# Sums over scan directions beside the dense convolutions: cut into pieces of two matmuls, spread over more half units, and charged to the TensorE budget of each half unit

## The chip, the cores and the metric

The kernel runs on one core of a Trainium2 chip. The metric is device time in microseconds (us), the median of several executions; lower is better. TensorE is called PE here, VectorE DVE, ScalarE ACT, GpSimd POOL, and SP is SyncE, which issues the DMAs.

## The reference, cut to what matters

Two layers of a vision network work on 8 images of 64 x 64 pixels and 192 channels, in float32. Layer 0 is a depthwise convolution, a chunked state-space scan in two directions and an MLP. Layer 1 splits the channels into halves: the left half goes through dense 3x3 convolutions, the right half through a selective scan in four directions over 192 inner channels with 16 states each:

```python
        # layer 1, left half
        y = _conv(_bn1(xl), conv1_w, conv1_b)
        y = _conv(relu(_bn2(y)), conv2_w, conv2_b)
        xl_out = relu(_conv(relu(_bn3(y)), conv3_w, conv3_b))
        ...
        # layer 1, right half: one recurrence for each of 4 directions, 192 channels, 16 states
        h = jnp.exp(d_t[..., None] * A) * h + (d_t * u_t)[..., None] * b_t[:, :, None, :]
        ys = einsum(h, c_t) + Ds * xs4
        yv = ys[:, 0] + jnp.flip(ys[:, 2], -1) + wh2hw(ys[:, 1]) + wh2hw(jnp.flip(ys[:, 3], -1))
        xr_out = einsum(_ln(yv) * silu(z), out_proj_w)
```

`yv`, the sum over the four directions with the skip term `Ds * xs4`, is what the change is about. `wh2hw` turns a plane walked by columns into one walked by rows.

## The kernel before

**The spine.** `selective_scan` (L1300 on) walks 3072 *units*, 384 for each image. A unit is one tile of 128 partitions (8 channels by 16 states) and 1024 tokens. For each unit SP fetches `dA` (L1435, 512 KB, six units ahead, seven buffers), ACT takes its exponential (L1440, two or three units ahead), PE spreads the inputs into `dB` in PSUM (L1448, two matmuls, two buffers), DVE weighs `dB` (L1465) and runs the scan instruction (L1472), POOL multiplies by C (L1475), and for every four units PE gathers the states into `acc` (L1486), which ACT copies to `y` (L1491). All of this is pinned: every engine takes its instructions in the order in which the Python code emits them, and SP's DMA issues stand in one queue in that order too.

**Work beside the spine.** All other work of an image is written as generators. A generator's `yield` of a number says how much TensorE work was just emitted (about one microsecond for 1.0, 1.2 for a 128x512 float32 matmul); a `yield None` says that nothing more of this generator is to be emitted in this half unit. `Beside.half()` runs twice in each unit: it adds `rate` to `credit` and then runs the generator in front until the credit is used up or a `None` comes. `rate` is set once per image in `spread_over`, from the sum of all the stages' costs. The scan's own matmuls are taken off the credit too (`beside.spend`).

The stages stand in this order beside the scan of image b: `conv0`, `ssd`, `mlp0` of image b+1 (layer 0), `conv_branch` of image b-2 (left half of layer 1), `scan_outputs` of image b-2, then `scan_inputs` and `transposed` of image b+1, which write `u`, the scan inputs of the next image, to DRAM. In the middle of the last but one tile of an image (unit 744 of the program, where the image ends at 768) `beside.finish()` emits at once whatever is left. Right behind it SP issues the loads of the next image's `u` (L1349), and three units later PE starts `ps_xp` from them (L1362). For the last image the list is `conv_branch`, `scan_outputs`, `conv_branch`.

**The sums.** `scan_sums` is a *side* generator: `conv_branch` sets it as `cx.side`, and from then on every half unit runs it up to its next `None` (`cx.aside()`). It works on 128 channels and then on 64. For each it loads the plane that is walked by columns into `whole` (for 128 channels POOL adds a second one to it, L1162), and then for each of 8 blocks of 512 tokens it puts the sum into one PSUM bank: plain matmuls with the identity or the skip diagonal (L1183: three for 128 channels, two for 64) and one matmul that reads `whole` with its rows and columns exchanged (L1185). ACT copies the bank out (L1188) and SP stores it (L1190). In the kernel before, all matmuls of a block are emitted in one half unit, and what they cost is counted nowhere: `aside()` drops the numbers, and `conv_branch=190.0` is the cost of the convolutions alone (8 blocks of 19 matmuls at 1.2). Such a side generator runs for images 0 to 6; the sums of image 7 stand in `tail()`, behind the scan.

Of the kernel before, what the change touches and what calls it, by code (L numbers as in the profile page):

```python
# [56 lines left out]
def wh_to_hw(ap):  # L57

    return ap.rearrange("p (w h) -> p h w", w=WW)
# [16 lines left out]
class Shared:  # L76
# [15 lines left out]

    def aside(self):

        for piece in self.side or ():
            if piece is None:
                return True
        self.side = None
        return False

    def pool(self, name, bufs=1):

# [180 lines left out]
def pause(n):  # L283

    for i in range(n):
        yield None


def among(gen, calls, n=2):

    calls = list(calls)
    for i, cost in enumerate(gen):
        yield cost
        if i % n == n - 1 and calls:
            calls.pop(0)()
    for call in calls:
        call()
        yield None
# [10 lines left out]
def token_rows(rows, d, c, n):  # L309

    width = 1
    for v in rows.shape[1:]:
        width *= v
    out = []
    for half in range(2):
        if d == 0:
            at, step, chunk = c * Q + half * Q // 2, 1, Q  # L320
        else:
            at, step, chunk = c * Q // HH + half, WW, Q // HH
        out.append((at * width, [[step * width, Q // 2], [chunk * width, n]]))
    return out
# [548 lines left out]
def conv_branch(cx, xl, short, out, side=None):  # L873

    nc, pin, k = cx.nc, cx.pin, cx.k
    with cx.pool("cw1") as wp, cx.pool("a1", 2) as ap:
# [78 lines left out]
        def load_w(i, r):  # L955
            here = slice(3 * r, 3 * (r + 1))
            pin(nc.sync.dma_start(out=ws[i][:, here], in_=k[("conv1_w", "conv2_w")[i]][:, here]))
# [11 lines left out]
        cx.side = side  # L969
        turns = in_turn(range(NB), scale, first, wait, second, third, add, store)  # L970
        yield from among(turns, [lambda r=r: load_w(1, r) for r in range(3)])
        while cx.aside():
            yield None


# [150 lines left out]
def scan_sums(cx, y, u):  # L1126

    nc, pin, k = cx.nc, cx.pin, cx.k

    def slots(n):  # L1130
        for i in range(n):
            yield 1.0
            yield None

    def cols(r, n):
        return slice(r * n, (r + 1) * n)

    with cx.pool("t2") as tp:

        for size, firsts, seconds, v, skip, eye in (  # L1140
            (128, [p[0] for p in y], [p[1] for p in y], u[0], k["skip_a"], k["ident"]),
            (64, [p[2][0:64] for p in y], [p[2][64:128] for p in y], u[2][0:64], k["skip_b"], k["twice"]),
        ):
            whole = tp.tile([128, L], F32, tag="whole", name="whole")
            for q in range(4):
                here = cols(q, L // 4)
                pin(nc.sync.dma_start(out=whole[:size, here], in_=seconds[0][:, here]))
                if size < 128:
                    pin(nc.sync.dma_start(out=whole[size:, here], in_=seconds[1][:, here]))
                yield from slots(1)  # L1150
            if size < 128:
                yield from slots(1)
            else:
                others = []
                for q in range(NB + 1):
                    if q < NB:
                        others.append(tp.tile([128, 512], F32, tag="p1", name="p1", bufs=2))
                        pin(nc.sync.dma_start(out=others[q], in_=seconds[1][:, cols(q, 512)]))
                    yield from slots(3 if q == 0 else 1)
                    if q > 0:  # L1160
                        here = cols(q - 1, 512)
                        pin(nc.gpsimd.tensor_add(whole[:, here], whole[:, here], others[q - 1]))  # L1162

            def load(r):
                part = tp.tile([128, 512], F32, tag="part", name="part", bufs=3)
                pin(nc.sync.dma_start(out=part[:size], in_=firsts[0][:, cols(r, 512)]))
                vt = tp.tile([size, 512], F32, tag="vt", name="vt", bufs=2)
                pin(nc.sync.dma_start(out=vt, in_=v[:, cols(r, 512)]))
                if size < 128:
                    pin(nc.sync.dma_start(out=part[size:], in_=firsts[1][:, cols(r, 512)]))  # L1170
                    return part, [(eye, part), (skip, vt)]
                p1 = tp.tile([128, 512], F32, tag="p1", name="p1", bufs=2)
                pin(nc.sync.dma_start(out=p1, in_=firsts[1][:, cols(r, 512)]))
                return part, [(eye, part), (eye, p1), (skip, vt)]

            coming = load(0)
            yield from slots(4)
            for r in range(NB):
                (part, terms), coming = coming, load(r + 1) if r + 1 < NB else None
                yield from slots(1)  # L1180
                ps = cx.one("ps_sum")[:size]
                for i, (w, t) in enumerate(terms):
                    pin(nc.tensor.matmul(ps, lhsT=w, rhs=t, start=i == 0, stop=False))  # L1183
                rows = wh_to_hw(whole)[:, r * RB : (r + 1) * RB, :]
                pin(nc.tensor.matmul(ps.rearrange("p (h w) -> p h w", w=WW), lhsT=eye, rhs=rows, start=False, stop=True))  # L1185
                yield 0.6 * len(terms)
                yield None
                pin(nc.scalar.copy(part[:size], ps))  # L1188
                yield from slots(1)
                pin(nc.sync.dma_start(out=firsts[0][:, cols(r, 512)], in_=part[:size]))  # L1190


# [72 lines left out]
class Beside:  # L1265
# [13 lines left out]

    def half(self):  # L1280

        self.cx.aside()
        self.credit = min(self.credit, self.rate) + self.rate
        while self.credit > 0.0 and self.stages:
            for cost in self.stages[0]:
                if cost is None:
                    return
                self.credit -= cost
                if self.credit <= 0.0:
                    return  # L1290
            self.stages.pop(0)
# [277 lines left out]
@with_exitstack  # L1569
def vision_mamba_pair_kernel(ctx: ExitStack, tc: tile.TileContext, x: bass.AP, p0: dict, p1: dict, out: bass.AP):  # L1570

    B = x.shape[0]
    cx = Shared(tc)
    cp = ctx.enter_context(tc.tile_pool(name="c", bufs=1))
    dp = ctx.enter_context(tc.tile_pool(name="d", bufs=1, space=DRAM))
    d2 = ctx.enter_context(tc.tile_pool(name="d2", bufs=2, space=DRAM))
    x1 = dp.tile([B, C, L], F32, tag="x1", name="x1")
    cx.singles = [ctx.enter_context(tc.tile_pool(name="ps", bufs=4, space=PSUM))]
    with cx.pool("once") as tp:
        setup(cx, cp, dp, tp, p0, p1)  # L1580
    us, ys, xns = {}, {}, {}

    def short(b):

        return x1[b].rearrange("(i g) l -> g i l", g=2)

    def sums(b):
        return scan_sums(cx, ys[b], us[b])

    def outputs(b):  # L1590
        return scan_outputs(cx, ys[b][0], xns[b], short(b)[1], out[b][1])

    def branch(b, side=None):
        return conv_branch(cx, x1[b][0:CH], short(b)[0], out[b][0], side)

    def stages(b):

        if b < B:
            us[b] = [d2.tile([128, L], F32, tag=f"u{t}", name=f"u{t}") for t in range(3)]
            ys[b] = [[d2.tile([128, L], F32, tag=f"y{g}{t}", name=f"y{g}{t}") for t in range(3)] for g in range(2)]  # L1600
            xns[b] = d2.tile([CH, L], F32, tag="xn", name="xn")
            beside.add(conv0(cx, x[b]))
            beside.add(ssd(cx))
            beside.add(mlp0(cx, x[b], x1[b]))
        if b > 1:
            beside.add(branch(b - 2, sums(b - 2)))
            beside.add(outputs(b - 2))
        if b == B:
            beside.add(branch(b - 1))
        if b < B:  # L1610
            beside.add(scan_inputs(cx, x1[b][CH:C], xns[b], us[b]))
            beside.add(transposed(cx, us[b]))

    beside = Beside(cx)
    with tc.tile_pool(name="ps_a", bufs=4, space=PSUM) as more:
        cx.singles.append(more)
        stages(0)
        beside.finish()
        beside.costs.update(conv_branch=190.0, scan_outputs=78.0)
        cx.singles.remove(more)  # L1620

    def tail():
        beside.add(sums(B - 1))
        beside.add(outputs(B - 1))
        beside.finish()

    def start_image(b, halves):
        stages(b + 1)
        beside.spread_over(halves, 450.0)

    selective_scan(cx, lambda b: us[b], lambda b: ys[b], beside, B, start_image, tail)
# [95 lines left out]
```

## Time and profile before

| | |
|---|---|
| time, median of 3 executions | 16043.01 us (16030.84, 16043.01, 16072.04) |
| the profiled execution | 16027.31 us |
| its span, first to last instruction | 16025.4 us |
| PE busy | 12969.3 us (81%) |
| DVE busy | 12232.0 us (76%) |
| POOL busy | 10981.2 us (69%) |
| ACT busy | 9059.2 us (57%) |
| DMA engines busy (queue of SP) | 79.5% of 16 engines' span |
| mean granted TensorE clock | 0.854 |

How to read it: the profile gives for each group of instructions its busy time, the mean duration of one, and how long its engine stood idle just before them and what ended that. A view by windows gives each engine's busy time in a stretch of the span, the granted PE clock (1.00 is full speed) and the mean busy share of the 16 DMA engines. A float32 matmul of the code shows as two matmul records in the profile. Matmuls are pipelined, so a busy PE is not a PE at its peak.

### The profile page before, as it was taken

How to read it: one execution, taken by the hardware profiler on the slowest of the kernel's cores; microseconds unless marked ns; L12 is line 12 of the kernel's file. 1: busy time of each engine (PE TensorE's matmuls, PEld its weight loads, DVE VectorE, ACT ScalarE, POOL GpSimd, SP SyncE). 2: the span in 40 equal slices, each digit the busy share in tenths (PEclk: the TensorE clock that was granted, in tenths of full speed). 3: DMA queues.
4: the chain of work that ended last, by engine and by line, in shares of the span. 5: the costliest groups of instructions: out<-in, count | busy, mean ns of one | idle time of the engine just before them, and what ended most of it. 6: DMA issues, size and time to landing. Idle time of an engine off the chain costs nothing. (4 is left out here: it accounts for less than half of the span.)

```text
span 16025.4 us, 207140 instructions
## 1 busy us (share of the span) xinstructions
PE 12969.3 (81%) x69608; PEld 4558.8 (28%) x69608; DVE 12232.0 (76%) x9262; ACT 9059.2 (57%) x13776; POOL 10981.2 (69%) x8165
## 2 busy tenths in 40 slices
PE   8977888789887898778878788787888778877766
PEld 4423322333223322233213332233322333211111
DVE  2268887887778877788678886788867887778994
ACT  3355566555665557655466565664656555655653
POOL 3258776876668766687667876678766776667783
PEclk9987888789887898878978799887988879879887
DMA  3288888878787887978878788887888878888885
GB/s 89 86 213 197 212 206 222 198 206 225 199 227 186 214 221 194 226 187 220 218 199 212 191 221 220 209 213 193 220 208 214 205 197 232 202 228 218 212 217 136
DMA packets 1604247, 3243.11 MB, mean 202 GB/s; under 512 B 389424, under 2 KB 843056, under 8 KB 1603184
## 3 DMA queue, kind: packets, MB, share of 16 engines
q1 hardware_dynamic: 1603184, 3229.84, 79.5%
q8 instruction: 556, 9.11, 0.3%
q14 instruction: 507, 4.15, 0.1%
HBM read 2550.93 MB, written 678.18 MB: 201 GB/s over the span
## 5 line engine op out<-in xcount | busy, mean ns | idle before, releaser
L1475 POOL TENSOR_TENSOR h<-h,bc 128x1024 f32<-128x1024 f32 x3072 | 7239.2, 2357 | 1334.9 <-DVE h L1472 1039.1
L1472 DVE TENSOR_TENSOR_SCAN h<-dA,carry,dB 128x1024 f32<-128x1024 f32 x3072 | 7200.3, 2344 | 479.5 <-ACT dA L1440 152.3
L1465 DVE TENSOR_TENSOR dB<-dB,bc 128x1024 f32<-128x1024 f32 x3072 | 3736.6, 1216 | 1665.2 <-PE dB L1448 1625.0
L1440 ACT ACTIVATE dA<-dA,neg_a 128x1024 f32<-128x1024 f32 x3072 | 3373.9, 1150 | 84.9 <-DMA dA<-dld 78.6
L1486 PE MATMUL acc<-h,gather 128*32 128x512 f32 x12288 | 2169.0, 703 | 319.0 <-POOL h L1475 134.7
L1474 POOL COPY carry<-h 128x1 f32<-128x1 f32 x2304 | 421.6, 183 | 2482.3 <-DVE h L1472 2344.5
L1448 PE MATMUL dB<-dus,spread 48*128 48x512 bf16 x6144 | 1401.2, 433 | 886.1 <-DVE h L1472 842.8
L1491 ACT COPY y<-acc 128x512 f32<-128x512 f32 x1536 | 890.2, 580 | 1842.1 <-issue 1014.9
L884 PE MATMUL ps_c<-p,conv_w 128*96 128x512 f32 x2304 | 1165.5, 628 | 37.3 <-ACT p L904 37.3
L1448 PEld LDWEIGHTS <-spread 48*128 48x128 bf16 x6144 | 321.2, 95 | 2969.5 <-issue 1374.7
L687 PE MATMUL ps_y<-X,M 64*64 64x64 f32 x12288 | 622.2, 277 | 433.3 <-issue 200.1
L336 PE MATMUL ps_cv<-pad,diag 64*64 64x512 f32 x6912 | 852.6, 606 | 19.6 <-ACT y L1491 13.0
L615 ACT ACTIVATE M<-ps_d,ln_dt 128x64 f32<-128x64 f32 x3072 | 666.5, 337 | 275.5 <-PE ps_d L621 206.8
L687 PEld LDWEIGHTS ps_y<-X,M 64*64 64x64 f32 x12288 | 567.7, 186 | 602.2 <-issue 256.5
L1486 PEld LDWEIGHTS acc<-h,gather 128*32 128x32 f32 x12288 | 290.7, 115 | 1223.3 <-issue 522.6
L609 ACT COPY bc<-ps_t 64x256 f32<-64x256 f32 x256 | 93.5, 365 | 917.1 <-PE ps_t L604 917.0
L620 PE MATMUL ps_d<-R,after 128*128 128x384 f32 x1024 | 572.7, 650 | 35.5 <-ACT bc L609 16.1
L1440 ACT ACT_TABLE_LOAD x445 | 570.9, 1283 | 7.9
L884 PEld LDWEIGHTS ps_c<-p,conv_w 128*96 128x96 f32 x2304 | 346.2, 167 | 721.9 <-issue 645.2
L1362 PE MATMUL ps_xp<-u,xp 128*128 128x512 f32 x768 | 471.1, 700 | 92.7 <-DMA u<-u 78.5
L1400 POOL TENSOR_TENSOR du<-dl,u 128x1024 f32<-128x1024 f32 x192 | 452.2, 2355 | 96.2 <-DMA bcd<-rows 81.0
L366 PE MATMUL ps_h<-oa,w1a 128*128 128x256 f32 x1536 | 456.0, 417 | 64.0 <-ACT y L1491 23.3
(248 smaller groups left out, 17979.2 us busy)
## 6 DMA issues: line engine op xcount, KB each, us to landing
dA<-dld SPq DMA_DIRECT2D x3072, 512.0 KB
dud<-terms SPq DMA_DIRECT2D x192, 768.0 KB
dus<-dud SPq DMA_DIRECT2D x1152, 128.0 KB
bc<-bcd SPq DMA_DIRECT2D x256, 512.0 KB
y<-yrows SPq DMA_DIRECT2D x256, 384.0 KB
u<-u SPq DMA_DIRECT2D x192, 512.0 KB
dld<-dl SPq DMA_DIRECT2D x192, 512.0 KB
y<-y SPq DMA_DIRECT2D x3072, 32.0 KB
```

Source lines behind the costliest of these rows:

```text
L336: pin(nc.tensor.matmul(ps[64 * b : 64 * (b + 1)].rearrange("p (h w) -> p h w", w=WW), lhsT=diag[:, t, :], rhs=pad[64 * i : 64 * (i + 1), b ...
L615: pin(nc.scalar.activation(M[:, d, h, :], ps[:, h * S : (h + 1) * S], AF.Exp, bias=bias))
L620: pin(nc.tensor.matmul(ps, lhsT=k["after"], rhs=flat(R[:, d * NH : (d + 1) * NH, :]), start=True, stop=False))
L687: pin(nc.tensor.matmul(psy[d][here, h * HP : (h + 1) * HP], lhsT=M[here, d, h, :], rhs=X[here, d, h, :], start=True, stop=True,))
L884: pin(nc.tensor.matmul(ps.rearrange("p (h w) -> p h w", w=WW), lhsT=w[:, t, :], rhs=pad[:, dy : dy + RB, dx : dx + WW], start=t == 0, stop ...
L1440: pin(nc.scalar.activation(dAs[q], dAs[q], AF.Exp, scale=k["neg_a"][:, steps[m][1], t, i : i + 1]))
L1448: pin(nc.tensor.matmul(dBs[q][:, half, :], lhsT=k["spread"][here, i % 2, :], rhs=du_of[n][here, i // 2, :], start=True, stop=True,))
L1465: pin(nc.vector.tensor_mul(dBs[q], dBs[q], of(q)[0]))
L1472: pin(nc.vector.tensor_tensor_scan(order(h, g), order(dA, g), order(dB, g), carry, ALU.mult, ALU.add))
L1475: pin(nc.gpsimd.tensor_mul(h, h, C_))
L1486: pin(nc.tensor.matmul(ps[32 * v : 32 * (v + 1)], lhsT=k["gather"], rhs=hs[q - 3 + v][:, here], start=True, stop=True))
L1491: pin(nc.scalar.copy(y[:, here], ps))
```

## The change

The sums' matmuls of a block are cut into two pieces, the first with two matmuls, the second with what is left (two for 128 channels, one for 64), with a `None` between. Each block waits three half units instead of one before its first piece. Each piece yields its cost (2.4, and 2.4 or 1.2), the plain waiting slots yield none any more (`pause`), `aside()` returns the cost of the piece it ran, and `half()` takes it off the credit. The cost of `conv_branch` is entered as 257.0, that is 190 and 67 for the sums; it holds for every `conv_branch`, the last one without sums too. What is computed, and the instructions, stay the same but for their order and for the ACT table loads, which the build places where the order of functions asks for them.

```diff
     def aside(self):
+        spent = 0.0
         for piece in self.side or ():
             if piece is None:
-                return True
+                return spent
+            spent += piece
         self.side = None
-        return False
+        return spent
...
-        while cx.aside():
+        while cx.side is not None:
+            cx.aside()
             yield None
...
-    def slots(n):
-        for i in range(n):
-            yield 1.0
-            yield None
...
-                yield from slots(1)
+                yield from pause(1)
...
             coming = load(0)
-            yield from slots(4)
+            yield from pause(4)
             for r in range(NB):
                 (part, terms), coming = coming, load(r + 1) if r + 1 < NB else None
-                yield from slots(1)
+                yield from pause(3)
                 ps = cx.one("ps_sum")[:size]
                 for i, (w, t) in enumerate(terms):
                     pin(nc.tensor.matmul(ps, lhsT=w, rhs=t, start=i == 0, stop=False))
+                    if i == 1:
+                        yield 2.4
+                        yield None
                 rows = wh_to_hw(whole)[:, r * RB : (r + 1) * RB, :]
                 pin(nc.tensor.matmul(ps.rearrange("p (h w) -> p h w", w=WW), lhsT=eye, rhs=rows, start=False, stop=True))
-                yield 0.6 * len(terms)
+                yield 1.2 * (len(terms) - 1)
                 yield None
                 pin(nc.scalar.copy(part[:size], ps))
-                yield from slots(1)
+                yield from pause(1)
                 pin(nc.sync.dma_start(out=firsts[0][:, cols(r, 512)], in_=part[:size]))
...
     def half(self):
-        self.cx.aside()
-        self.credit = min(self.credit, self.rate) + self.rate
+        self.credit = min(self.credit, self.rate) + self.rate - self.cx.aside()
...
-        beside.costs.update(conv_branch=190.0, scan_outputs=78.0)
+        beside.costs.update(conv_branch=257.0, scan_outputs=78.0)
```

More of the change, by code (lines that the diff above doesn't have):

```diff
@@ L1158, in scan_sums @@
                         pin(nc.sync.dma_start(out=others[q], in_=seconds[1][:, cols(q, 512)]))
-                    yield from slots(3 if q == 0 else 1)
+                    yield from pause(3 if q == 0 else 1)
                     if q > 0:
@@ L1183, in scan_sums @@
                     pin(nc.tensor.matmul(ps, lhsT=w, rhs=t, start=i == 0, stop=False))
+                    if i == 1:
+                        yield 2.4
+                        yield None
                 rows = wh_to_hw(whole)[:, r * RB : (r + 1) * RB, :]
                 pin(nc.tensor.matmul(ps.rearrange("p (h w) -> p h w", w=WW), lhsT=eye, rhs=rows, start=False, stop=True))
-                yield 0.6 * len(terms)
+                yield 1.2 * (len(terms) - 1)
                 yield None
                 pin(nc.scalar.copy(part[:size], ps))
-                yield from slots(1)
+                yield from pause(1)
                 pin(nc.sync.dma_start(out=firsts[0][:, cols(r, 512)], in_=part[:size]))
```

## The prediction, made before the changed kernel ran

> **What bounds the kernel now.** I read the page first (span, engines, costliest groups), then windows cut where the first matmul of each stage stands, then the waits inside two of them, then the timeline at an image's end.
>
> ```profile
> PE 12969.3 (81%) x69608; PEld 4558.8 (28%) x69608; DVE 12232.0 (76%) x9262; ACT 9059.2 (57%) x13776; POOL 10981.2 (69%) x8165
> ...
> L1472 DVE TENSOR_TENSOR_SCAN h<-dA,carry,dB 128x1024 f32<-128x1024 f32 x3072 | 7200.3, 2344 | 479.5 <-ACT dA L1440 152.3
> L1465 DVE TENSOR_TENSOR dB<-dB,bc 128x1024 f32<-128x1024 f32 x3072 | 3736.6, 1216 | 1665.2 <-PE dB L1448 1625.0
> ```
>
> No engine is full over the span. DVE owes each unit 2344 + 1216 ns = 3.56 us, and its largest idle time by far is 1625.0 us before L1465, for `dB` from PE. So time is lost where PE has more than a unit's worth of work in front of `dB`. Where that is, one image period shows (image 4):
>
> ```profile
> 6482.70:6787.30 304.60, 266.33 (x1948) 98.34 (x1947) 267.20 (x155) 213.72 (x301) 226.24 (x165) 0.94 0.91 227
> 6787.30:7310.90 523.60, 393.22 (x3180) 170.48 (x3178) 424.63 (x430) 259.51 (x602) 429.40 (x358) 0.76 0.76 187
> 7310.90:7709.20 398.30, 353.47 (x1674) 151.18 (x1671) 342.48 (x242) 253.77 (x336) 285.22 (x172) 0.94 0.85 223
> 7709.20:8006.60 297.40, 269.79 (x758) 73.66 (x756) 192.54 (x110) 125.71 (x159) 178.15 (x145) 0.96 0.88 223
> 8006.60:8342.90 336.30, 288.45 (x1048) 68.97 (x1044) 259.37 (x185) 252.22 (x299) 214.09 (x159) 0.81 0.74 188
> 8342.90:8421.20 78.30, 37.59 (x105) 9.04 (x106) 41.84 (x25) 35.22 (x35) 39.03 (x20) 0.63 0.95 247
> ```
>
> Columns: stretch, length, busy us of PE, weight loads, DVE, ACT, POOL, granted PE clock, DMA share, GB/s. The rows are conv0, ssd, mlp0, conv_branch with the sums, scan_outputs with scan_inputs, and the image's end; they hold 76, 88, 89, 54, 65 and 12 units (counted in the instruction order: pairs of L1448 between first matmuls). In the branch PE is busy 91% and DVE 65%, a unit takes 297.4/54 = 5.51 us. Elsewhere DVE is at 77 to 88% (53% at the end). The waits of DVE in the branch and at the end:
>
> ```profile
> DVE dB L1465 <- PE dB L1448: 91.8, 35, 9.1
> ...
> DVE dB L1465 <- PE dB L1448: 19.9, 2, 16.4
> DVE h L1472 <- ACT dA L1440: 14.7, 1, 14.7
> ```
>
> 91.8 us of idle DVE per branch are what the change can win. And within the branch, the 28 units with sums:
>
> ```profile
> L1185 PE MATMUL ps_sum<-whole,twice 128*64 128x512 f32 x16 | 15.3, 1042 | 0.0
> L1185 PE MATMUL ps_sum<-whole,ident 128*128 128x512 f32 x16 | 15.0, 1027 | 0.0
> L1183 PE MATMUL ps_sum<-part,ident 128*128 128x512 f32 x16 | 8.9, 641 | 3.1 <-DMA part<-y 1.6 <-issue 1.5
> ```
>
> A plain matmul of the sums (two records) takes 8.9/8 = 1.1 us of PE, one on `whole` 1.9. A block of 128 channels is 3 x 1.1 + 1.9 = 5.2 us in one half unit, on top of about 1.9 us of convolution.
>
> **The change, part by part.** *Nothing is removed*: PE, DVE, POOL and DMA work stay the same. The build holds 1378 ACT table loads instead of 1355; at 1283 ns each (page, L1440) 30 us of ACT. ACT is 42% busy in the branch and DVE waits for its `dA` 1.8 us there, so I cost them at nothing; uncovered they would be 30 us in all.
>
> *What moves.* `rate` goes from 450/768 + 1140.8/705 = 2.20 to 450/768 + 1207.8/705 = 2.30 per half unit: every other stage is packed denser, and the branch, now charged for the sums, is stretched. The order of the two programs gives units per image: conv0 76 to 72, ssd 88 to 90, mlp0 89 to 83, branch 54 to 70 (the sums' matmuls over 50 instead of 27), outputs and scan_inputs 65 to 62, image's end 12 to 7. This holds for six images. So what counts is what a unit costs when it is added to or taken from a stage. At least its own PE work: (2169.0 + 1401.2 + 471.1 + 318.0)/3072 = 1.42 us (L1486, L1448, L1362, L1394). Where DVE paces, 325.7/91 = 3.58 us (the scan alone, 15459 to 15785).
>
> *Branch, +16.* PE work becomes 269.8 + 16 x 1.42 = 292.5 us, 4.18 per unit. Two evenly fed stretches tell the pace: conv0 with 266.3/76 = 3.50 us of PE per unit takes 4.01, and ten units of scan_inputs (8287.0 to 8336.8: 47.02 us of PE) with 4.70 take 4.98. A straight line (slope 0.81) gives 4.56 at 4.18: 70 x 4.56 = 319, **+22**. Bounds: PE without a gap, 292.5 (-5); 16 units at 3.58 (+57). DMA has to be asked too: 0.88 x 297.4 = 262 us of full engines, and 16 units bring 0.80 x 325.7/91 = 2.86 each, 308 in all. That fits in 319 at a share of 0.97. The stretch 7769 to 7821 shows 0.99 at 268 GB/s, so it can be carried, with no room left.
>
> The Trainium skill has a rule that would take this worry away ("DMA: Bandwidth & Descriptors", Specifications): it puts the HBM limit of a core at about 358 GB/s. By it the branch's 223 GB/s x 297.4 us + 16 x 0.70 MB = 77 MB would need an estimated 216 us, and DMA could not bind. The trace's engines are full at 268 GB/s with these packets, so the row is used.
>
> *conv0, -4.* (266.3 - 5.7)/72 = 3.62 of PE; the line gives 4.11 x 72 = 296: **-9** (-6 at 1.42 each, -16 at 4.01).
>
> *mlp0, -6.* The line's slope gives (4.475 + 0.81 x 0.18) x 83 = 384: -14. Image 0 ran this stage with 104 units in 464.1 us, 4.46 each, the same pace as 89 units; so the time may just go with the units, -27. I take the middle, **-20** (-8.5 to -27).
>
> *ssd, +2.* Image 0 ran it with 101 units in 553.4 us: 29.8 us for 13 more, 2.3 each, **+5** (+3 to +12).
>
> *Outputs and scan_inputs, -3*: between 1.42 and 3.58 each, **-7.5** (-4 to -11).
>
> *Image's end, -5* units at 41.84/12 = 3.5 of DVE: **-17**. But its stalls stay, and one grows. In the kernel before, `transposed` came to its end by itself two units before `finish()`: ACT did six copies, two exponentials, then two copies. Now the order shows all eight copies (1.9 us each) and eight stores emitted by `finish()`, straight in front of SP's loads of the next `u`. The timeline now:
>
> ```profile
> 8362.47 3.73 ACT L1114 COPY part<-whole 64x1024 f32<-64x1024 f32 x2 [3.93 <-DMA whole<-u]
> ...
> 8368.28 2.35 DVE L1472 TENSOR_TENSOR_SCAN h<-dA,carry,dB 128x1024 f32<-128x1024 f32 x1 [14.74 <-ACT dA L1440]
> ...
> 8372.96 0.45 SPq L1123 DMA_DIRECT2D u<-part  x1
> ...
> 8378.30 0.34 SPq L1349 DMA_DIRECT2D u<-u  x1
> ...
> 8397.05 0.50 PEld L1362 LDWEIGHTS ps_xp<-u,xp 128*128 128x128 f32 x2 [4.04 <-DMA u<-u]
> ```
>
> DVE waits 14.74 us for exponentials that stand behind the copies; two more copies less the 1.04 us cast that stood among them add 2.8. SP had 5.3 us between the last store and the first load of `u`, in which stands one unit's work; now the loads follow at once, and PE, which takes L1362 in its order in front of the next `dB`, waits for them longer, some 4 us. Queued behind on SP: the `dA` fetches of six units ahead, which have that lead; behind L1362 on PE: `dB`, and so DVE. Together **+7** (0 if ACT's gaps swallow it; +24 if all from that store, 8372.96, to PE's last wait, 8397.05, is uncovered).
>
> *Sum per image:* 22 - 9 - 20 + 5 - 7.5 - 17 + 7 = about -20; six images -120 (-122 unrounded).
>
> *Last image.* Its stages hold 116, 52, 118 and 91 units (branch, outputs, branch, scan alone: 488.5, 232.7, 441.3, 325.7 us). They become 131, 44, 96 and 106, since the last branch is charged 257 for 190. Branch: (381.5 + 21.3)/131 = 3.07 of PE; between the second branch (2.71, 3.74) and conv0 (3.50, 4.01) that is 3.86, +17. Outputs 8 fewer at the low end, -11. Second branch 3.84 x 96, -72. Alone 15 x 3.58, +54. **-12** (-35 to +19).
>
> Total -134: 16027 - 134 = 15893 against the profiled execution. The median shown lies 16 us above that execution; on its scale 15909, I say **15910**.
>
> **Rivals.** *The image's end takes it back.* If the eight copies, stores and loads run in a row with nothing under them, +24 stands for +7: -3 per image, -32 in all, 16011, no change. For it: DMA share 0.95 there, SP in order. Against: the lead of six `dA`s.
>
> *DMA becomes the bound of the branch.* If the engines can't be kept fuller than the 0.88 they show now, because SP's queue stops at stores that wait for a copy (L1190 in this queue), the branch takes 308/0.88 = 349, +52 for +22, and the last image's first branch (0.90 x 488.5 + 15 x 2.86)/0.90 = 536, +48 for +17: +10 per image, +19 at the end, 16043 + 78 = 16121, slower. It decides from a branch of some 348 us. For it: 262 to 308 us of transfers. Against: 0.99 in places, and smaller pieces shorten the wait of those stores.
>
> *More is won.* PE runs the branch almost without gaps (+5) and mlp0 goes with its units (-27): -44 per image, 15765. For it: 26 us stretches with PE busy 26.00. Against: the branch's first 11 units (7709 to 7767) leave PE 19% idle now, before any sum.
>
> **How the numbers follow.** A measurement can tell about 0.3%, 48 us, from no change. Forecast 0.55, of which 0.05 ends within 0.3%; image's end 0.14; DMA 0.18; more won 0.13. Faster 0.50 + 0.13 = 0.63, same 0.19, slower 0.18. The range leaves out half of the DMA case and the lower half of the last: 15760 to 16110.
>
> **What would show it.** In the branch 70 units, DVE's wait for `dB` falling from 91.8 to about 70 us, length near 319, DMA share near 0.97; L1183 and L1185 in alternating short bursts. mlp0 near 380 us, conv0 near 296. At the image's end one DVE wait on ACT of 14 to 18 us and longer waits of L1362 on `u`. The forecast is wrong if the branch is over 340 us, or if the stalls at the end grow by more than 24.

## The result, and the profile after

The changed kernel takes 16121.86 us (median of 8 executions) against 16032.67 us of the kernel before in the same comparison: ratio 1.0055 [1.0044, 1.0067], slower by 0.55%, where 15910 was predicted. The profiled execution took 16093.2 us, its span is 16091.4 us, 66 us above that of before.

First the page, engines and groups:

```profile
PE 12940.8 (80%) x69608; PEld 4560.9 (28%) x69608; DVE 12235.7 (76%) x9262; ACT 9096.4 (57%) x13799; POOL 10983.1 (68%) x8165
...
L1472 DVE TENSOR_TENSOR_SCAN h<-dA,carry,dB 128x1024 f32<-128x1024 f32 x3072 | 7199.8, 2344 | 521.2 <-ACT dA L1440 200.3
L1465 DVE TENSOR_TENSOR dB<-dB,bc 128x1024 f32<-128x1024 f32 x3072 | 3737.1, 1216 | 1584.0 <-PE dB L1448 1562.0
...
L1362 PE MATMUL ps_xp<-u,xp 128*128 128x512 f32 x768 | 482.6, 717 | 288.1 <-DMA u<-u 283.9
```

The work is the same but for 23 more ACT instructions, the table loads (13799 for 13776): DVE's busy time is within 4 us, ACT's is 37 us more and PE's 28.5 us less, for the same number of matmuls. DVE's idle time before `dB` fell by 81 us (1665.2 to 1584.0), before the scans it rose by 42, and PE now waits 283.9 us for `u` where it waited 78.5. So the wait that the change aimed at did shrink, and its gain went elsewhere. Where, the windows show, cut for image 4 at the same six places as before (same columns; a row runs from the scan of the first unit of a stage to the scan of the first unit of the next):

```profile
6510.30:6817.20 306.90, 265.95 (x1928) 97.09 (x1927) 254.24 (x147) 208.16 (x295) 214.31 (x156) 0.93 0.87 217
6817.20:7354.30 537.10, 405.69 (x3180) 174.70 (x3178) 432.54 (x435) 260.54 (x602) 436.48 (x366) 0.74 0.76 185
7354.30:7747.90 393.60, 348.17 (x1639) 150.79 (x1639) 321.64 (x230) 248.83 (x329) 265.69 (x156) 0.93 0.85 215
7747.90:8069.00 321.10, 287.17 (x858) 76.88 (x856) 247.67 (x143) 153.47 (x189) 227.78 (x182) 0.94 0.94 242
8069.00:8385.70 316.70, 258.87 (x1023) 63.16 (x1022) 248.22 (x179) 247.50 (x294) 205.42 (x148) 0.88 0.75 190
8385.70:8457.40 71.70, 28.50 (x79) 7.73 (x80) 24.60 (x14) 28.34 (x27) 22.36 (x13) 0.61 0.92 230
```

In conv0 (first row) and mlp0 (third row) DVE has 13 and 21 us less to do than before, because four and six units have gone, and yet the rows are nearly as long as before (306.9 for 304.6, 393.6 for 398.3). DVE's freed time has become idle time: over six images its wait for `dB` grew from 21 to 35 us in conv0 and from 39 to 58 in mlp0. The same cut for six images (images 2 to 7 of the program) gives the means that all later runs are compared by; units per image are counted in the instruction order:

| kernel | conv0 | ssd | mlp0 | branch | outputs, scan_inputs | end | image |
|---|---|---|---|---|---|---|---|
| before: units | 76 | 88 | 89 | 54 | 65 | 12 | 384 |
| before: us | 304.6 | 525.5 | 396.0 | 296.2 | 333.2 | 75.6 | 1931.2 |
| after: units | 72 | 90 | 83 | 70 | 62 | 7 | 384 |
| after: us | 306.4 | 535.3 | 394.3 | 321.0 | 317.7 | 70.4 | 1945.2 |
| difference, us | +1.8 | +9.8 | -1.7 | +24.8 | -15.5 | -5.2 | +14.0 |
| predicted, us | -9 | +5 | -20 | +22 | -7.5 | -10 | -20 |

Six times +14 and the last image's -18 (1586.1 to 1567.9 us) make the 66 us of the two spans. The end of image 4, in the view of waits (engine, line, what it waited for: us in total, times, longest):

```profile
PE ps_xp L1362 <- DMA u<-u: 33.3, 3, 28.4
...
DVE dB L1465 <- PE dB L1448: 27.1, 3, 15.7
DVE h L1472 <- ACT dA L1440: 20.0, 3, 18.9
```

and in the timeline (start, length, engine, line; in brackets the idle time ahead):

```profile
8401.00 7.37 ACT L1117 COPY part<-whole 128x1024 f32<-128x1024 f32 x4 [11.81 <-DMA whole<-u]
...
8410.25 7.36 ACT L1117 COPY part<-whole 64x1024 f32<-64x1024 f32 x4 [1.87 <-DMA whole<-u]
...
8419.22 2.35 DVE L1472 TENSOR_TENSOR_SCAN h<-dA,carry,dB 128x1024 f32<-128x1024 f32 x1 [18.91 <-ACT dA L1440]
```

All eight copies of `transposed` now stand in a row, behind an ACT wait of 11.81 us for the load of `whole`; the exponentials are behind them, DVE waits 18.91 us (14.74 before). In the branch the wait of DVE that was the target:

```profile
DVE dB L1465 <- PE dB L1448: 58.1, 29, 12.5
```

58.1 us for 91.8, over 70 units instead of 54.

### The profile page after: what moved, and what is told of

It is laid out like the page before. It is cut to its first block, busy times and chain, and to the rows that moved or that the text cites. A ratio compares the mean times of both kernels' runs of the same rounds, so it can differ in the third digit from the quotient of the medians.

```text
span 16091.4 us, 207144 instructions
## 1 busy us (share of the span) xinstructions
PE 12940.8 (80%) x69608; PEld 4560.9 (28%) x69608; DVE 12235.7 (76%) x9262; ACT 9096.4 (57%) x13799; POOL 10983.1 (68%) x8165
## 5 line engine op out<-in xcount | busy, mean ns | idle before, releaser
L1465 DVE TENSOR_TENSOR dB<-dB,bc 128x1024 f32<-128x1024 f32 x3072 | 3737.1, 1216 | 1584.0 <-PE dB L1448 1562.0
L1440 ACT ACTIVATE dA<-dA,neg_a 128x1024 f32<-128x1024 f32 x3072 | 3377.2, 1151 | 135.4 <-DMA dA<-dld 125.4
L1486 PE MATMUL acc<-h,gather 128*32 128x512 f32 x12288 | 2136.3, 698 | 314.2 <-POOL h L1475 130.2
L1362 PE MATMUL ps_xp<-u,xp 128*128 128x512 f32 x768 | 482.6, 717 | 288.1 <-DMA u<-u 283.9
L1440 ACT ACT_TABLE_LOAD x474 | 608.1, 1283 | 8.5
```

Source lines behind the costliest of these rows:

```text
L1440: pin(nc.scalar.activation(dAs[q], dAs[q], AF.Exp, scale=k["neg_a"][:, steps[m][1], t, i : i + 1]))
L1465: pin(nc.vector.tensor_mul(dBs[q], dBs[q], of(q)[0]))
L1486: pin(nc.tensor.matmul(ps[32 * v : 32 * (v + 1)], lhsT=k["gather"], rhs=hs[q - 3 + v][:, here], start=True, stop=True))
```

## The experiments

All stage figures below are means per image like those of the table, from one profiled execution of each kernel. Whole-run ratios are given where a kernel was executed four times or more; the others are one execution each.

**1. The parts of the change, one at a time.** The denser rate alone, on the kernel before:

```diff
-        beside.costs.update(conv_branch=190.0, scan_outputs=78.0)
+        beside.costs.update(conv_branch=257.0, scan_outputs=78.0)
```

> Only conv_branch=257.0 in the kernel before: the rate rises to 2.30, the sums stay whole and uncharged. Units per image: conv0 72, ssd 90, mlp0 83, branch 52, outputs and scan_inputs 63, image's end 24. Theory A (denser stages do not get shorter): conv0 306, ssd 535, mlp0 394 us as in the changed kernel, the image's end longer by some 45 us, image period about 1970, time about 16250. Theory B (the loss is made in the branch, by its pieces and its 70 units): conv0 and mlp0 go with their units, about 296 and 375, the period stays near 1931, time about 16030.

Measured: 16336.18 us, ratio 1.0197 [1.0182, 1.0213], slower than either theory said. conv0 takes 306.8 with 72 units, mlp0 393.8 with 83: what the changed kernel shows too. What follows: the two stages do not shorten when units are taken from them, and nothing of the sums' new form is needed for that. The units that they lose pile up at the image's end (24 units, 120.6 us), because the charge is never used, and the branch takes 307.9 us with 52 units, longer than before with 54.

The pieces alone, on the kernel before, uncharged:

```diff
                     pin(nc.tensor.matmul(ps, lhsT=w, rhs=t, start=i == 0, stop=False))
+                    if i == 1:
+                        yield None
```

> Only a None after the second matmul of a block in the kernel before: pieces, no charge, rate 2.20, units of all stages as before, sums' matmuls over 35 instead of 27 units. Theory A: other stages as before, branch 5 to 20 us shorter than 296, time 15930 to 16000. Theory B: branch not shorter than 296, time 16030 or more.

Measured: 16026.80 us, 1.0002 [0.9991, 1.0012]; the branch 298.9 us with 54 units. The pieces alone do nothing; that the branch would get shorter was a miss, and the numbers are nearly those of Theory B, whose account of the loss the denser rate alone (above) and the own rate (experiment 2) contradict.

The charge with whole blocks, on the changed kernel:

```diff
-                yield from pause(3)
+                yield from pause(1)
...
-                    if i == 1:
-                        yield 2.4
-                        yield None
...
-                yield 1.2 * (len(terms) - 1)
+                yield 1.2 * (len(terms) + 1)
```

> The changed kernel with the sums' blocks whole again (one half unit for all matmuls, one waiting slot), but charged, 257: units per stage as in the changed kernel. Theory A: conv0 306, ssd 535, mlp0 394 again, branch 321 to 335, time 16100 to 16200. Theory B: branch under 318 us, time under 16080.

Measured: 16183.63 us, 1.0104 [1.0086, 1.0122]; the branch 331.1 us with the same 70 units. Once the sums are charged, pieces with their longer spacing (three waiting half units for one, which this run took back together with them) are worth 10 us per branch. So of the change's parts the dense rate costs, and the pieces give something back.

**2. The charge where it is used.** If the stages away from the sums gain nothing from a denser rate, they should keep the old one, and only the half units that run a sum should get more. On the changed kernel, with `conv_branch=190.0` again:

```diff
-        self.rate = own / halves + work / (halves - 9 * len(self.stages))
+        share = work / (halves - 9 * len(self.stages))
+        self.plain = own / halves + share
+        self.full = own / halves + share * 257.0 / 190.0
...
+        beside_sums = self.cx.side is not None
+        self.rate = self.full if beside_sums else self.plain
```

> The changed kernel's pieces and charge, but the higher rate only while the sums run (2.78 there, 2.20 elsewhere). Units: conv0 76, ssd 88, mlp0 89 as before, branch 58, outputs and scan_inputs 63, end 10. Theory A: conv0 305, ssd 525, mlp0 396, branch 290 to 300, time 15930 to 16020. Theory B: branch 25 us longer than 296, time about 16090.

Measured: 15917.31 us, 0.9934 [0.9914, 0.9954] to the kernel before: faster than both and a little below its range. conv0, ssd and mlp0 are back at 76, 88 and 89 units with 305.7, 528.9 and 394.3 us. The branch holds 58 units in 295.1 us, which is four more than before in the same time. The gain stands behind it: outputs and scan_inputs take 314.6 us with 63 units (333.2 with 65 before), and the last image is 29 us shorter. Why two units fewer are worth 18.6 us there, no run singles out. With three output buffers and one shortcut buffer in the branch as well, so that ACT waits less for the store of the rows before:

```diff
-            os[r] = ap.tile([CH, 512], F32, tag="o", name="o")
+            os[r] = ap.tile([CH, 512], F32, tag="o", name="o", bufs=3)
...
-            shs[r] = ap.tile([CH, 512], F32, tag="sh", name="sh")
+            shs[r] = ap.tile([CH, 512], F32, tag="sh", name="sh", bufs=1)
```

> The run with its own rate in the branch, and three buffers instead of two for the branch's output tile (one instead of two for the shortcut tile). ACT waits 25 us per image there for the output's store. If that wait is on the path: branch 280 to 288 instead of 295, time 15820 to 15880. If it is not: branch within 4 us of 295, time within 0.2% of 15917.

Measured: 15904.18 us, 0.9917 [0.9894, 0.994]; the branch 294.2 us. ACT's wait for that store, 22.3 us in the branch of image 4, is gone, and the branch is 1 us shorter: that store is not what holds it, and the two versions can't be told apart. The windows of the version with more buffers, branch and outputs of image 4:

```profile
7687.70:7981.90 294.20, 273.67 (x783) 75.31 (x782) 208.22 (x118) 134.41 (x168) 191.34 (x156) 0.94 0.93 234
7981.90:8296.90 315.00, 262.71 (x1027) 64.16 (x1029) 251.75 (x180) 246.84 (x294) 208.00 (x153) 0.87 0.80 195
```

PE is busy 93% of the branch here (91% before, 89% in the changed kernel): with 58 units its gaps are smaller than with 54 or 70.

**3. How far the floor reaches.** The other way round: the other stages at 0.93 of the old share and the branch at 1.8 times.

```diff
+        self.plain = own / halves + share * (0.93 if len(self.stages) == 7 else 1.0)
+        self.full = own / halves + share * (1.8 if len(self.stages) == 7 else 257.0 / 190.0)
```

> Pieces, charge and a rate of its own while the sums run, as in the run with its own rate, but the other stages at 0.93 of their share and the branch at 1.8 times: conv0 80 units, ssd 95, mlp0 93, branch 52, outputs and scan_inputs 60, end 4. A (a knee near 72 to 76 units of conv0 and 83 to 89 of mlp0: below it the time stays, above it each unit costs DVE's 3.6 us): conv0 305 + 4 x 3.6 = 319, mlp0 394 + 4 x 3.6 = 409, ssd 525 + 7 x 5.9 = 566, time above 16050. Rival (a straight line of some 2.3 us per unit, as the prediction had it): conv0 314, mlp0 405.

Measured: 16405.21 us. conv0 takes 321.7 us with 80 units, mlp0 435.9 with 93. Beside conv0, 71 to 76 units cost 305 to 307 us in every run with its work and the old charges, and four more cost 16 (4.0 each): a floor with a knee near 76, just where the kernel before stood. The last units of this window hold no matmul of conv0 any more; up to conv0's last matmul the picture is the same, 272.2 us with 69 units before, 272.6 with 65 in the changed kernel, 291.5 with 74 here. The number of units is not all, though: a run of experiment 5 that changed nothing in conv0 (own rate, new charges in mlp0) took 315.0 us there with 76 units, and nothing on record says why. mlp0 lengthened more than was expected, which no run explains.

**4. Another allowance at the end.** Ten half units of slack for each stage in place of nine:

```diff
-        self.rate = own / halves + work / (halves - 9 * len(self.stages))
+        self.rate = own / halves + work / (halves - 10 * len(self.stages))
```

> The changed kernel with 10 instead of 9 half units of allowance per stage in the rate (2.316 for 2.299), so that the last copies of the transposed plane are emitted in two groups with exponentials between, as in the kernel before, and not all in front of the next image's loads. If the end's stalls cost what the flush makes them cost: outputs, scan_inputs and end together 388 falls by 8 to 12 us per image, time about 16060. If not: within 4 us, time 16120 to 16140.

Measured: 16175.02 us, 1.0075 [1.0059, 1.0091]. Outputs and the image's end together take 395.0 us (388.1 in the changed kernel): the gain that was expected there did not come, although the copies did go out in two groups with exponentials between them, as in the kernel before. DVE's idle time at the end itself fell by 3 us only (45.8 to 43.1). So the row of eight copies is a small part of the loss.

**5. What paces mlp0.** First PE: 10 of 18 narrow matmuls (L795) of each pass left out of the result, some 20 us of PE, after and before.

```diff
-                for b, low in enumerate(lows):
+                for b, low in enumerate(lows if f in (0, n - 1) else ()):
```

> The changed kernel with 10 of the 18 small matmuls that contract to the last 64 channels in each of mlp0's 8 passes left out (their yields stay, so units and half units are the same: mlp0 83); by L793 of the kernel before, 0.25 us each, 20 us less PE work in mlp0 per image. Theory A1 (the stage is paced by PE: its time is PE's work plus gaps): mlp0 394 falls to 374, DVE's idle time in it from 73 to about 53 us. Theory A2 (paced by something that goes with the stage's steps: ACT's queue, PSUM banks, DMA): mlp0 stays within 5 us of 394.

> The same matmuls left out of the kernel before: mlp0 89 units, rate 2.20. A1: mlp0 396 falls by 8 to 20 us, less than in the changed kernel, since DVE comes to pace it. A2: within 5 us of 396.

Measured: 16133.83 us with mlp0 at 392.0 (after), 16031.21 with 396.1 (before). Narrow matmuls pace neither, though less went than was meant: PE's busy time in the stage fell by 16 us (349.4 to 333.0) and by 10 (350.0 to 339.8). Then evenness: the stage's costs set in proportion to the PE time of each piece, on the changed kernel and on the version of experiment 2.

```diff
-                        yield 1.8
+                        yield 2.1
...
-                yield 1.2
+                yield 1.0
...
-                yield 0.6
+                yield 0.52
```

> The changed kernel, and in mlp0 the charges set in proportion to PE's measured time: 2.1 for 1.8 (the two wide products), 1.0 for 1.2 and 0.52 for 0.6 (the narrow ones), 1.05 for 1.2 (the transposes); the sum stays 282 to 283, so mlp0 keeps 83 units and all others theirs. Theory A3 (mlp0 does not shrink because PE is over-full in its wide products, 5.46 us per unit, while its narrow ones run at DVE's pace, 4.08, whatever the rate): mlp0 falls from 394 to 365 to 385, DVE's idle time in it from 73 to some 50. Theory A4 (it is ACT's queue and the PSUM banks that hold PE): mlp0 within 5 us of 394.

> The run with its own rate while the sums run, with the same charges in mlp0 (89 units). A3: mlp0 396 falls by 5 to 20 us, less than at 83 units, since DVE is nearer to pacing it; time 15800 to 15890. A4: within 5 us, time within 0.3% of 15917.

Measured: 16234.64 us, 1.0111 [1.0092, 1.0129], mlp0 412.3; and 16031.77 us, 0.9989 [0.9979, 0.9998], mlp0 402.9. Both stages got longer, which neither theory had. Giving units by PE time makes the stage longer: PE time is not what a unit waits for there. ACT is the other engine in it, and it had more to do: it switched its function tables (ACT_TABLE_LOAD) 58 times an image in this stage where the changed kernel does 51 times, and 54 times where the version of experiment 2 does 49 times. (The count alone does not give the length: the run of experiment 4 has 46 and 399.0 us with 84 units.) The costliest groups of ACT in mlp0 of the changed kernel:

```profile
L1440 ACT ACTIVATE dA<-dA,neg_a 128x1024 f32<-128x1024 f32 x84 | 91.9, 1142 | 0.3
L822 ACT ACTIVATE h<-ps_h,b 128x256 f32<-128x256 f32 x96 | 37.6, 474 | 34.4 <-PE ps_h L370 34.2
L1440 ACT ACT_TABLE_LOAD x26 | 33.4, 1283 | 0.5
...
L822 ACT ACT_TABLE_LOAD x13 | 16.7, 1283 | 0.2
...
L766 ACT ACT_TABLE_LOAD x7 | 9.0, 1283 | 0.1
```

The scans' exponentials and the Silu of the wide products (L822) and of the gate (L766) come by turns, and each turn loads a table for 1283 ns: 51 an image (49 before), of which 12 (10) go with the scans' own inputs and stay when Silu goes. In the changed kernel PE waits in mlp0 for those Silu copies, which free the PSUM banks of the wide products. The line of the wide products on the two pages, before and after:

```profile
L366 PE MATMUL ps_h<-oa,w1a 128*128 128x256 f32 x1536 | 456.0, 417 | 64.0 <-ACT y L1491 23.3
L368 PE MATMUL ps_h<-oa,w1a 128*128 128x256 f32 x1536 | 478.9, 433 | 88.0 <-ACT h L822 46.2
```

Identity in place of Silu takes the switches away; the activations of conv0, gate and wide products are then missing from the result:

```diff
-                            h1[:, f + n, b, :], ps[:, n * T : (n + 1) * T], AF.Silu, bias=k["b1"][:, f + n : f + n + 1]
+                            h1[:, f + n, b, :], ps[:, n * T : (n + 1) * T], AF.Identity, bias=k["b1"][:, f + n : f + n + 1]
```

> The changed kernel with Identity in place of Silu in the wide products and the gate of the first MLP stage and in the first depthwise convolution, so ScalarE need not switch its tables there between the exponentials and Silu; the activations themselves are left out of the result. Units per stage as in the changed kernel. Theory S (ScalarE paces: table loads of 1283 ns, 51 in the MLP stage and 37 in the convolution stage, stand between the exponentials and the evictions that TensorE waits for): the MLP stage falls from 394 to 360-375 us an image, the convolution stage from 306 to 290-300, the whole to 15770-15930. Theory T (TensorE's wide products pace): both stages within 5 us of 394 and 306, whole 16060-16150.

> The kernel before with the same Identity in place of Silu; the activations are left out of the result. Theory S: the MLP stage 396 falls by less than in the changed kernel if the density of the scans is what brings ScalarE to its limit (to 375-390), the convolution stage 305 to 295-302. Theory T: both within 5 us of 396 and 305; whole 15980-16060.

Measured: after 15957.23 us, mlp0 369.7 (394.3 with Silu); before 15945.77 us, mlp0 387.1 (396.0). The windows of mlp0 in image 4, without the switches, after:

```profile
7296.00:7663.70 367.70, 335.79 (x1636) 146.22 (x1637) 320.95 (x231) 194.42 (x289) 265.14 (x156) 0.96 0.91 230
```

and before:

```profile
7258.30:7644.60 386.30, 349.54 (x1668) 150.04 (x1669) 341.83 (x242) 202.15 (x297) 285.07 (x172) 0.95 0.90 232
```

DVE's work is what it was in both; its wait for `dB` in this stretch is 36.6 us in the changed kernel without switches,

```profile
DVE dB L1465 <- PE dB L1448: 36.6, 30, 7.5
```

where it was 57.7 with them. So in mlp0 the switches are what kept six fewer units from saving time: without them 83 units are 17.4 us shorter than 89. Half of the 24.6 us that the changed kernel gained here are shorter matmuls (415 ns for 435 in the first of the wide products' two lines): PE's busy time fell from 349.4 to 337.0 us at a granted clock of 0.96 for 0.92, while before it stayed (350.0 and 350.3, 0.95 both). The switches are all that was changed in this stage (an Identity of the wide products takes 477 ns, a Silu 474), so they are the cause; how the waits and the clock act on each other was not tested. conv0 did not answer: 306.1 and 302.6, and the whole time of the changed kernel missed its range by 27 us. Last, the second matmul of each wide product left out (64 of the 192 rows that are summed), about 34 us of PE:

```diff
-    for b, (out, x) in enumerate(zip(outs, xbs)):
+    for b, (out, x) in enumerate(zip(outs, xbs) if whole else ()):
...
-                    product(cx, [ps[:, at] for ps in pss], w1, cols, *both(*os[i]))
+                    product(cx, [ps[:, at] for ps in pss], w1, cols, *both(*os[i]), whole=False)
```

> The changed kernel with the second matmul (64 rows) of each wide product of the first MLP stage left out: 96 matmuls of about 0.35 us an image, some 34 us of TensorE work, in the units that have become longest. Units per stage as in the changed kernel. Theory S (ScalarE paces): the MLP stage stays within 5 us of 394. Theory T (TensorE's wide products pace): it falls to 360-370 us, the whole to about 15930-15970.

Measured: 16002.67 us, mlp0 380.4, between the two theories. The windows of mlp0 in image 4:

```profile
7284.60:7665.90 381.30, 324.29 (x1447) 139.68 (x1447) 320.55 (x230) 249.58 (x329) 265.40 (x156) 0.90 0.87 221
```

PE's busy time fell by 24 us here (348.17 to 324.29), 26 in the mean, not by 34, at a granted clock of 0.90 for 0.93; the stage gave back 14. The wide products are made and copied out by turns: ACT waits for PE's `ps_h` (34.2 us in the rows above) and PE for ACT's `h`. What was taken from either side of that loop shortened the stage.

**6. What paces conv0.** Two of nine taps of its convolution left out of the result, 24 us of PE, after and before, and then after without Silu too:

```diff
-        for i, (ps, diag) in enumerate(zip(pss, diags)):
+        for i, (ps, diag) in enumerate(zip(pss, diags) if t not in skip else ()):
```

> The changed kernel with two of the nine taps of the first depthwise convolution left out: 192 of 864 matmuls an image, 24 us of TensorE work by their row (107.1 us for 864), not charged otherwise, so units per stage stay as they are (72 beside this convolution). Theory T (TensorE's work paces this stage in the changed kernel): the stage falls from 306 to 280-290 us an image and the whole to 15930-15990. Theory Q (the scans with their ring, or ScalarE's evictions, pace it): it stays within 5 us of 306.

> The kernel before with the same two taps left out, 76 units beside the convolution. Theory T with the scans already near their own pace (76 units at the 3.74 us that a unit with short waits takes are 284): the stage falls from 305 to 290-300. If both engines bind it equally in turn, it falls by 5-15. Theory Q: it stays within 5 us of 305.

> The changed kernel with the two taps and, as in the earlier run, the Silu left out of the first convolution, the wide products and the gate. If TensorE alone paces the convolution stage, it is as without the taps alone, within 4 us. If ScalarE's table switches stand right behind TensorE's work, it falls by another 5-15 us. The MLP stage stays at 370 either way.

Measured: conv0 307.8, 306.5 and 305.3 us; whole 16111.01, 16026.75 and 15948.01. In the first of them PE's busy time in the stage fell by 11 us only (265.4 to 254.3), not by 24, at a granted clock of 0.90 for 0.93; in the second by 8, at 0.90 for 0.94. In the last PE is relieved of 14 us and ACT of 32, and the stage is 1 us shorter. So this much of PE's matmuls, of ACT's switches or of both does not pace the stage; what it would be at an unchanged clock, these runs can't tell. In the last of these runs ACT's longest waits ahead of the copies of the projected rows (L461) are for their store; in the view of that line (what its engine sat idle for: us, times):

```profile
L461 ACT COPY po<-ps_p x256: 268/281/317, 91.6 to 12481.4; 128x140 f32<-128x140 f32 x128
...
  DMA prows<-po: 141.5, 39
```

The changed kernel itself waits there less often:

```profile
L461 ACT COPY po<-ps_p x256: 250/282/316, 95.3 to 12622.3; 128x140 f32<-128x140 f32 x128
...
  DMA prows<-po: 68.6, 25
```

A third buffer on top of the run without taps and Silu (the last two taps left out this time, whose weights make the room):

```diff
-            po = vp.tile([128, 2, 2 * NP0], F32, tag="po", name="po")
+            po = vp.tile([128, 2, 2 * NP0], F32, tag="po", name="po", bufs=3)
```

> The changed kernel without the Silu (convolution, wide products, gate) and without two of the nine taps of the first convolution (the last two instead of the fourth and sixth), as in the run before it, and with three buffers instead of two for the projected rows of that convolution, whose copies on ScalarE wait for the store of the rows before (141 us in the whole run before it, 17 us an image). Theory R (that wait, which stands at the head of ScalarE's queue, holds the stage): the convolution stage falls from 305 to 290-299 us an image, the whole from 15948 to 15860-15910. Otherwise (the hand-overs between the engines in order, no single one): within 4 us of 305.

Measured: 15914.71 us, conv0 298.5 (305.3); the line's view has no wait for the store any more. The stage falls, just inside the range of the theory, while the whole is 5 us above its own. So this wait holds some 7 us, once PE and ACT are relieved, if the choice of the two taps makes no difference, which was not tried alone. What keeps the rest from going down to the 72 x 3.56 = 256 us of DVE's own work stays open: no run singled it out, and the third buffer wasn't tried on the stage with its work left in.

## Why the prediction was wrong

**The step that failed** is the cost of a unit taken away: "The line's slope gives (4.475 + 0.81 x 0.18) x 83 = 384", "I take the middle, -20" for mlp0, and "the line gives 4.11 x 72 = 296: -9" for conv0. That line was drawn through two different stages, and image 0, whose 104 units took 4.46 us each, was taken as a sign that the time goes with the units below 89 too. Measured: -1.7 and +1.8, 29 us per image or 175 of the 200 us between the 15893 of the sum and the 16093 of the profiled execution. Experiment 1 shows this part by itself, with the sums untouched. The range of both terms did not hold "no gain" either; the bounds, -8.5 and -6, took a unit's own PE work, 1.42 us, as the least that it can save. Not even that came off PE: its busy time went from 350.0 to 349.4 us in mlp0 and from 265.8 to 265.4 in conv0, and the granted clock from 0.95 to 0.92 and from 0.94 to 0.93. In outputs and scan_inputs it was the other way, 286.7 to 264.3 us for three units fewer, at 0.86 for 0.81. The prediction held PE's time for the rest of a stage fixed, and it was not. Its own signs of being wrong, a branch over 340 us and stalls up by more than 24, did not show; of its signs of being right, mlp0 near 380 us and conv0 near 296 failed.

In mlp0 the cause was shown: ACT's table switches. With them gone, the difference between 89 and 83 units is -17.4, near the -20 of the forecast. The prediction had counted the table loads and passed them by ("I cost them at nothing") as 23 additional ones in the branch; it was those that had always been in mlp0 (49 an image, now 51) which came to the front when the stage was packed denser. In conv0 the cause stays open; the store of the projected rows is a part, found in a relieved stage only.

**ssd, +5**: +9.8, inside its bounds (+3 to +12) at 4.9 us a unit and so nearer to the end where a unit costs the stage's mean of 6.0. **Branch, +22**: +24.8, right in the units (70), in the DMA share (0.94 for 0.97) and in DVE's wait for `dB`, which fell (58.1; some 70 forecast). The size came from the same line as the two failed terms, so that it fits is partly luck; with the sums whole the same 70 units gave +34.9. **Outputs and scan_inputs, -7.5**: -15.5, beyond the -11 of its range. The denser rate alone has it too (316.3 us with 63 units), so it does not come from the pieces. It is 5 us a unit, more than the 3.58 that was taken for the most. But the run of experiment 3 took 333.2 us with 60 units, so it does not simply go with the units either: the cause is open. **Image's end, -10**: -5.2. The stall has the sign and the place that were told, and is larger: DVE's wait on ACT is 18.9 us at its longest in image 4 (18.0 to 21.0 over the six images, 14.3 to 17.0 before), just above the 14 to 18 forecast, and PE's waits for `u` grew from 78.5 to 283.9 us over the run, 29 an image over seven images. DVE's idle time at the end grew by 12 us an image (33.7 to 45.8), where 7 were counted. **Last image, -12**: -18.

**The rivals.** DMA as the bound of the branch gave 16121 us, the time that was measured, by coincidence, for its mechanism did not happen: the branch took 321.0 us, not 349, and the engines went to 0.94. "More is won" and the rival at the image's end did not happen either. No rival named the stages that get denser; one that says "the stages that lose units keep their length" was missing: 22 + 5 - 7.5 - 10 = +9.5 per image and -12 at the end make 16027 + 45 = 16072 for the profiled execution, 16088 on the scale of the median.

**What the change was worth.** Its aim was sound: charged and in pieces, the sums give the branch units at a fair price (16 for 24.8 us, 1.55 each). But the units were taken from the wrong place, by one rate for the whole image. With the extra rate only while sums run it is 0.66% faster than before instead of 0.55% slower.

## What to carry to other kernels

Before counting a gain from packing a stage denser, find its floor: run the same stage with two or three densities, because here a line through two different stages missed it. When side work is charged to a budget, charge it where it runs; a rate that is spread over everything takes units from stages that can't use the room. And look at the loops of two engines (product, copy out, freed bank), not only at how full each engine is: no engine was full in mlp0, and a switch of 1.3 us in such a loop held it back. Nor is an engine's busy time a fixed amount of work: here PE's moved with the granted clock when only the order or the density had changed.

## What the hardware showed that was not expected

Each table load takes 1283 ns with 18 ns of idle time ahead of it (474 at L1440 with 8.5 us in all, on the page after). 39 fewer of them an image took 54.3 us from ACT's busy time in mlp0 (248.8 to 194.5), 1.39 us each, and 24.6 us from the stage when it was packed densely; when it was not, 51.8 us (253.8 to 202.0), 1.33 each, and 8.9 from the stage. The Trainium skill ("ScalarE: Activation LUTs", What ACT_TABLE_LOAD costs) gives 1283 ns for the load, which agrees, and a further 1380 ns of drain for every switch, which these rows do not show.
